# A graph layer on one core: running sums by fours, a further product per block of counts, and a subtraction on GpSimd

## The chip, the core and the metric

One core of a Trainium2 chip runs the whole layer in one launch. It has five engines that work side by side, each through its own queue in order: TensorE (PE; its weight loads are listed apart as PEld), VectorE (DVE), ScalarE (ACT), GpSimd (POOL) and SyncE (SP), which here only starts transfers. Engines wait for each other by semaphores. The metric is the device time of one execution in microseconds, lower is better; of several executions the median counts.

## What is computed

A layer of a graph network with 6250 nodes of 256 features and 106,250 directed edges `src`, `dst`, sorted by `dst`:

```
xn = layernorm(x)
x  = x + gnn(xn, edges) + mix(xn)      # mix: linear attention over all nodes
x  = x + ffn(layernorm(x))             # 8 experts, 2 per node

def graph_conv(x, edges, W0, b0, W1, b1):       # twice, relu between
    s = concatenate([edges[:, 0], edges[:, 1]])
    d = concatenate([edges[:, 1], edges[:, 0]])
    deg = maximum(segment_sum(ones_like(d), d, N), 1)
    agg = segment_sum(x[s], d, N) / deg[:, None]
    return x @ W0 + b0 + agg @ W1 + b1
```

The change lies in the part that comes first. There the edges are sorted into a table of places, from which the next stage builds the adjacency matrix block by block, and the nodes are normalised and split into a high and a low half, so that the sums over neighbours can be taken as products with the adjacency on TensorE.

## The kernel before

Nodes are cut into 49 blocks of 128 (`NB`), and twelve groups of four blocks and one of one (`NGRP`). For each block a window of 19 x 128 edges is read (`Q` = 19 columns of 128 edges). Two blocks are handled as a pair, two pairs as a batch: 13 batches, the last with one pair.

The front is one large stretch of code whose order on the engines is written out by hand: in `manual_schedule` TensorE, VectorE, ScalarE and SyncE run their instructions in the order in which Python emits them. Generators are interleaved step by step for that; a `yield` is a step. The main loop (`for b in range(NBAT)`) steps through `assign(b)` and after each of its steps takes one step of `count(b + 1)`, one of the edge preparation `edges(k)` (every other batch) and, as far as a budget goes, one of `left`, which holds the node groups `nodes(g)` and behind them the attention `mixing()`. What stands in a queue therefore depends on how many steps each generator has.

`count(b)` makes the counts of a batch. It compares the edges' keys with the numbers of the blocks (L414): `hot` is a one-hot of 100 numbers for each edge column, 19 columns per pair. It adds neighbouring columns to nine pair sums `sofar` (L423) and then runs a sum over these, eight additions of 2 x 100 elements on VectorE (L426), each reading the one before. Afterwards it issues the first three `rank_of`.

`rank_of(b, m)` puts the ranks of four (or at the end three) columns into one of three buffers `rk` in the TensorE's result memory: a product with `mark` (order within a column, and a large number at the edge's own place, L398), one or two with a matrix of ones over `sofar` (all columns before, L402), and one over the even columns of `hot` for the odd ones (L407). There are ten such counts for each full batch.

`assign(b)` takes the maximum of each count on VectorE (L438), which frees its buffer, and issues `rank_of` three further on. Then follow some small operations, and for each pair five routes (L467, comparisons into 128 x 1024 elements), four carries (L476) and their products on TensorE (L490), whose results ScalarE copies to `place`. Before the routes of each pair `own_term` is called twice (L243, products of the node group with a weight; ScalarE adds a bias, L246).

`nodes(g)` normalises a group: statistics on VectorE (L257, L260), square root on ScalarE (L265), reciprocal and offset on VectorE (L268, L269), the normalised nodes and their rounded high halves on ScalarE (L273, L276). Then come transposes on TensorE (L285), the low halves, a subtraction on VectorE (L289, normalised minus high), and the Gram products for the attention (L294). At its end the load of the group two further on is issued on SyncE's queue (L74).

GpSimd has only index patterns and the first edge loads to do in the front; the weight loads of the next stage (L642) stand in its queue behind.

Of the kernel before, what the change touches and what calls it, by code (L numbers as in the profile page):

```python
# [8 lines left out]
F32 = mybir.dt.float32  # L9
# [6 lines left out]
ENG = mybir.EngineType  # L16
PSUM = bass.MemoryType.PSUM
DRAM = bass.MemoryType.DRAM
P = 128
# [3 lines left out]
Q = 19  # L23
# [16 lines left out]
def tile_gps_layer(ctx: ExitStack, tc: tile.TileContext, a, out):  # L40
    nc = tc.nc
    x, src, dst = a["x"], a["src"], a["dst"]
    N, D = x.shape
    E = src.shape[0]
    F = a["W0_0"].shape[1]
    NE, _, FE = a["W1e"].shape
# [7 lines left out]
    J = NB + 1  # L54
# [12 lines left out]
    def blocks(g):  # L67
        return range(g * T, min(NB, g * T + T))
# [33 lines left out]
    onesb = const.tile([P, P], BF16, name="onesb")  # L102
# [32 lines left out]
    with ExitStack() as p1:  # L135
# [87 lines left out]
        if NB % 2:  # L223
            nc.vector.memset(eds[:, NP - 1, :, 1], 0)

        p1.enter_context(tc.manual_schedule(engines={ENG.PE, ENG.DVE, ENG.Activation, ENG.SP}))

        def load_nodes(g):
            load_rows(xns[g % XB][:, :, :D], blocks(g), nc.sync)
# [4 lines left out]
        def own_term():  # L234

            if not owed:
                return
            g, f, xnT = owed.pop(0)
            bs = blocks(g)
            n = len(bs)  # L240
            tp = pt1.tile([P, T * P], F32, name="tp")
            for c in range(DC):
                nc.tensor.matmul(tp[:, :n * P], w00[:, c, f * P:(f + 1) * P],  # L243
                                 xnT[:, c, :n * P], start=(c == 0), stop=(c == DC - 1))
            own = (wq, wfc)[f % 2].rearrange("p c d -> p (c d)")
            nc.scalar.activation(own[:, :n * P], tp[:, :n * P], AF.Identity, bias=bh[:, f:f + 1])  # L246
            nc.scalar.dma_start(self_d[f, :, bs[0] * P:(bs[-1] + 1) * P], own[:, :n * P])

        def nodes(g):

            bs = blocks(g)
            n = len(bs)
            xn = xns[g % XB]
            st = wk.tile([P, T, nc.vector.BN_STATS_DIM], F32, name="st")
            mv = wk.tile([P, T, nc.vector.BN_AGGR_DIM], F32, name="mv")
            for i in range(n):
                nc.vector.bn_stats(st[:, i, :], xn[:, i, :D])  # L257
                yield
            for i in range(n):
                nc.vector.bn_aggr(mv[:, i, :], st[:, i, :])  # L260
                yield
            sd = wk.tile([P, T], F32, name="sd")
            rs = wk.tile([P, T], F32, name="rs")
            off = wk.tile([P, T], F32, name="off")
            nc.scalar.activation(sd[:, :n], mv[:, :n, 1], AF.Sqrt, bias=eps)  # L265
            for _ in range(3):
                yield
            nc.vector.reciprocal(rs[:, :n], sd[:, :n])  # L268
            nc.vector.scalar_tensor_tensor(off[:, :n], mv[:, :n, 0], -1.0, rs[:, :n], op0=OP.mult,  # L269
                                           op1=OP.mult)  # L270
            yield
            for i in range(n):
                nc.scalar.activation(xn[:, i, :D], xn[:, i, :D], AF.Identity, bias=off[:, i:i + 1],  # L273
                                     scale=rs[:, i:i + 1])
            part = sent[:, bs[0]:bs[-1] + 1]
            nc.scalar.copy(part[:, :, 0], xn[:, :n, :D])  # L276
            for _ in range(5):
                yield
            while owed:
                own_term()  # L280
            xnT = wk.tile([P, DC, T * P], F32, name="xnT", bufs=1)
            for c in range(DC):
                tp = pt1.tile([P, T * P], F32, name="tp")
                for i in range(n):
                    nc.tensor.transpose(tp[:, i * P:(i + 1) * P], xn[:, i, c * P:(c + 1) * P], ident)  # L285
                nc.scalar.copy(xnT[:, c, :n * P], tp[:, :n * P])
                yield
            nc.scalar.dma_start(xnT_d[:, :, bs[0] * P:(bs[-1] + 1) * P], xnT[:, :, :n * P])
            nc.vector.tensor_sub(part[:, :, 1], xn[:, :n, :D], part[:, :, 0].bitcast(F32))  # L289
            yield  # L290

            for i, b in enumerate(bs):
                for c in range(DC):
                    nc.tensor.matmul(gram[:, GW[c]:GW[c] + W - c * P], xn[:, i, c * P:(c + 1) * P],  # L294
                                     xn[:, i, c * P:], start=False,
                                     stop=(b == NB - 1 and c == DC - 1))
                yield
            if g + XB < NGRP:
                load_nodes(g + XB)
            owed.extend((g, f, xnT) for f in range(FC))  # L300
            if g < EARLY:
                while owed:
                    own_term()
                    yield
# [77 lines left out]
        def of_batch(b):  # L382

            k, i = divmod(b, PK // PB)
            n = min(PB, NP - b * PB)
            key, pay, *rest = facts[k]
            s = slice(i * PB, i * PB + n)
            return n, key[:, s], pay[:, s], *(t[:, s] for t in rest)
# [3 lines left out]
        def rank_of(b, m):  # L392

            hot, sofar = hots[b]
            i, (q0, q1) = m // len(QS), QS[m % len(QS)]
            pp = pr.tile([P, 4, J * 2], F32, name="rk")
            h = hot[:, i].rearrange("p q j r -> p q (j r)")
            nc.tensor.matmul(pp[:, :q1 - q0], mark, h[:, q0:q1], start=True, stop=False)  # L398

            for q, d in ((2, 2),) if q0 == 0 else ((q0, 4),) if q1 - q0 == 4 else ((q0, 2), (q0 + 2, 1)):  # L400
                s, e = q // 2 - 1, max(1, d // 2)
                nc.tensor.matmul(  # L402
                    pp[:, q - q0:q - q0 + d].rearrange("p (s e) j -> p s e j", s=e), onesb,
                    sofar[:, i, s:s + e, None, :].to_broadcast([P, e, d // e, J * 2]),
                    start=False, stop=False)
            n = (q1 - q0) // 2
            nc.tensor.matmul(pp[:, 1:2 * n:2], onesb, h[:, q0:q0 + 2 * n:2], start=False, stop=True)  # L407
            ranks[b, m] = pp[:, :q1 - q0].rearrange("p q (j r) -> p q r j", r=2)

        def count(b):  # L410

            n, key, *_ = of_batch(b)
            hot = wk.tile([P, PB, Q, J, 2], BF16, name="hot")
            nc.vector.tensor_tensor(  # L414
                hot[:, :n].rearrange("p a q j r -> p (a q) j r"),
                jdx[:, None].to_broadcast([P, n * Q, J, 2]),
                key.rearrange("p a q r -> p (a q) r")[:, :, None, :].to_broadcast([P, n * Q, J, 2]),
                op=OP.is_equal)
            yield
            sofar = wk.tile([P, PB, Q // 2, J * 2], BF16, name="sofar")  # L420
            hots[b] = hot, sofar
            h = hot.rearrange("p a q j r -> p a q (j r)")
            nc.vector.tensor_add(sofar[:, :n], h[:, :n, 0:Q - 1:2], h[:, :n, 1:Q:2])  # L423
            yield
            for q in range(1, Q // 2):
                nc.vector.tensor_add(sofar[:, :n, q], sofar[:, :n, q - 1], sofar[:, :n, q])  # L426
                yield
            for m in range(min(3, n * len(QS))):
                rank_of(b, m)

        def assign(b):
# [4 lines left out]
            for m in range(n * len(QS)):  # L436
                i, (q0, q1) = m // len(QS), QS[m % len(QS)]
                nc.vector.tensor_reduce(rank[:, i, q0:q1], ranks.pop((b, m)), AX.X, OP.max)  # L438
                if m + 3 < n * len(QS):
                    rank_of(b, m + 3)  # L440
                yield
# [154 lines left out]
        for _ in nodes(0):  # L596
            pass
        first_edges = edges(0)
        for _ in nodes(1):
            next(first_edges, None)  # L600
        for _ in first_edges:
            pass
        for _ in count(0):
            pass
        left = chained(*(nodes(g) for g in range(EARLY, NGRP)), mixing())
        per_round = -(-(NGRP - EARLY) * 26 // max(1, NBAT - 2))
        for b in range(NBAT):
# [291 lines left out]
    with ExitStack() as p2:  # L899
# [36 lines left out]
        for g in range(NGRP):  # L936
            bs = blocks(g)
            n = len(bs)
# [18 lines left out]
            for i, b in enumerate(bs):  # L957
                ts = slice(i * P, (i + 1) * P)
                pb = py.tile([P, 512], F32, name="pb")
                for c in range(DC):  # L960
                    nc.tensor.matmul(pb[:, :D], xnT[:, c, ts], wmix[:, c, :],
                                     start=(c == 0), stop=False)
                for f in range(FC):
                    nc.tensor.matmul(pb[:, :D], hT[f][:, ts], w["W0_1"][:, f, :], start=False,
                                     stop=(f == FC - 1))
                nc.vector.tensor_add(bt[:, i], bt[:, i], pb[:, :D])
                pz = py.tile([P, 512], F32, name="pz")
                for f in range(FC):
                    nc.tensor.matmul(pz[:, :D], hT[f][:, ts], w["W1_1"][:, f, :], start=(f == 0),
                                     stop=(f == FC - 1))  # L970
# [67 lines left out]
    with ExitStack() as p3:  # L1038
# [200 lines left out]
        for t in range(len(steps) + AH):  # L1239
# [5 lines left out]
            if t >= AH:  # L1245
                g, j = steps[t - AH]
# [6 lines left out]
        for _ in running:  # L1253
# [37 lines left out]
                         stop=True)  # L1291
# [174 lines left out]
```

## Time and profile before

| | us |
|---|---|
| median of 3 executions (2476.81 to 2477.54) | 2476.87 |
| profiled execution | 2479.15 |
| its span, first to last instruction | 2477.5 |
| PE busy in the span | 2312.7 |
| DVE busy | 1535.1 |
| ACT busy | 991.2 |
| POOL busy | 346.9 |
| running sums L426: 96 of 2 x 100 elements, mean 0.254 | 24.4 |
| reductions L438: 100 of 4 columns, mean 0.564 | 56.2 |
| subtractions L289: 12 of 1024 elements, mean 1.219 | 14.6 |
| products L402: 75 of 400, 50 of 200, 25 of 100 columns | 48.4 |

The first rows are of the whole kernel, the last four of the front. Busy times add up the lengths of instructions; the next one of an engine can start before the end of the one before, so a mean is somewhat longer than the distance of starts. The front ends when the first comparison of the next stage (L693) starts on VectorE at 370.8 us.

### The profile page before, as it was taken

Reading aid. Unit: us, or ns where it says so; the run is one execution under the profiler, and the core shown is the slowest. Engines: PE = TensorE matmul, PEld = TensorE weight load, DVE = VectorE, ACT = ScalarE, POOL = GpSimd, SP = SyncE. Lnnn points to the kernel's source line nnn. Section 1 sums busy time; section 2 is a strip of 40 time slices with the busy share of each in tenths; the row PEclk is TensorE's granted clock in tenths of the full one; section 3 lists DMA queues with packets and bytes.
Section 4 is the critical chain, followed back from the end, with each engine's and each line's share of the span. In section 5 each row is a group of like instructions: output and inputs, shape, how many; then the busy total and the mean of one; then the engine's idle time right before and its main releaser. Section 6 shows DMA issues by size and latency. Waiting matters only on the chain. (4 is left out here: it accounts for less than half of the span.)

```text
span 2477.5 us, 44108 instructions
## 1 busy us (share of the span) xinstructions
PE 2312.7 (93%) x13401; PEld 1817.9 (73%) x13401; DVE 1535.1 (62%) x4304; ACT 991.2 (40%) x2805; POOL 346.9 (14%) x372
## 2 busy tenths in 40 slices
PE   5788869999999999989999899999999987999996
PEld 3455547777777777767777778877878766999985
DVE  5999988888888888863333334444444443655554
ACT  2344425555555555541111133333433433544443
POOL 1000000000000000000000101211121122555554
PEclk9899989999999999999999999999999987999998
DMA  3232273333333333334333264544454435778885
GB/s 107 67 102 88 83 243 131 110 107 107 110 109 112 110 110 110 111 97 172 111 124 124 88 222 160 169 153 168 160 177 148 166 111 183 230 217 244 247 250 161
DMA packets 258653, 359.24 MB, mean 145 GB/s; under 512 B 46840, under 2 KB 192895, under 8 KB 258278
## 3 DMA queue, kind: packets, MB, share of 16 engines
q1 hardware_dynamic: 229890, 302.64, 37.9%
q0 software_dynamic: 16384, 32.82, 4.0%
q10 hardware_dynamic: 12132, 20.86, 2.3%
q8 instruction: 111, 1.82, 0.3%
q14 instruction: 136, 1.11, 0.1%
HBM read 209.88 MB, written 160.00 MB: 149 GB/s over the span
## 5 line engine op out<-in xcount | busy, mean ns | idle before, releaser
L663 PE MATMUL sum<-adj,sent 128*128 128x512 f32 x2352 | 623.6, 407 | 0.0
L1077 PE MATMUL sum<-sent,adj 128*128 128x512 f32 x2401 | 580.5, 401 | 15.4 <-DVE adj L1055 14.4
L1077 PEld LDWEIGHTS sum<-sent,adj 128*128 128x128 f32 x2401 | 451.1, 190 | 125.7 <-DVE adj L1055 11.2
L714 ACT ACTIVATE adj<-pt 128x512 fp32r<-128x512 f32 (+1 forms) x637 | 359.2, 571 | 337.3 <-PE pt L711 332.2
L663 PEld LDWEIGHTS sum<-adj,sent 128*128 128x128 f32 x2352 | 420.6, 189 | 79.6
L693 DVE TENSOR_TENSOR oh<-iota,place 128x1024 bf16<-128x1024 bf16 (+1 forms) x686 | 402.1, 630 | 88.4 <-PE pt L711 86.5
L1053 ACT CAST adj<-many 128x512 fp32r<-128x512 bf16 (+1 forms) x318 | 185.5, 595 | 329.4 <-PE sum L1077 242.2
L1055 DVE CAST adj<-many 128x512 fp32r<-128x512 bf16 (+1 forms) x319 | 130.0, 414 | 247.9 <-PE sum L1077 192.7
L721 DVE CAST kept<-adj 128x512 bf16<-128x512 f32 (+1 forms) x637 | 231.7, 406 | 6.3 <-ACT adj L714 5.1
L1347 PE MATMUL pm<-yT,w 128*128 128x128 f32 x1616 | 201.9, 279 | 8.0 <-ACT yT L1331 7.3
L711 PEld LDWEIGHTS <-oh 128*128 128x128 bf16 x2548 | 148.0, 98 | 82.5 <-DVE kept L721 61.2
L711 PE MATMUL pt<-oh 128*128 128x128 bf16 x2548 | 200.1, 221 | 0.6 <-DVE misfit L633 0.6
L1347 PEld LDWEIGHTS pm<-yT,w 128*128 128x128 f32 x1616 | 191.4, 194 | 11.7 <-ACT yT L1331 10.5
L1359 PE MATMUL po<-w2e,hT 128*128 x808 | 193.9, 383 | 4.6 <-ACT hT L1351 4.6
L1359 PEld LDWEIGHTS po<-w2e,hT 128*128 128x128 f32 x808 | 147.7, 193 | 21.3 <-ACT hT L1351 5.0
L1006 POOL IOTA home_i<- 128x8 int32 x1 | 0.1, 130 | 1042.5 <-SPq L785 1042.5
L1351 ACT ACTIVATE hT<-pm,b 128x128 f32<-128x128 f32 x404 | 115.7, 372 | 50.2 <-PE pm L1347 23.1
L1210 POOL DMA_INDIRECT lists<-rows,place_i x98 | 97.1, 991 | 269.1 <-DVE rows L1202 223.0
L714 ACT ACTIVATION_READ_ACCUMULATOR adj<-pt 128x1 f32 x637 | 127.0, 199 | 0.0
L1380 POOL DMA_INDIRECT got<-ybuf,at x101 | 106.3, 1053 | 119.7 <-DMA ybuf<-res 61.7
L1363 ACT ACTIVATE res<-res,row 128x256 f32<-128x256 f32 x101 | 51.3, 508 | 163.1 <-DVE res L1362 104.9
L1395 POOL DMA_INDIRECT out_dram<-both,at x101 | 102.3, 1013 | 88.9 <-DVE both L1393 68.2
(264 smaller groups left out, 2508.9 us busy)
## 6 DMA issues: line engine op xcount, KB each, us to landing
adjd<-kept SPq DMA_DIRECT2D x588, 128.0 KB
many<-adjd SPq DMA_DIRECT2D x84, 896.0 KB
w<-in_W1e_dram SPq DMA_DIRECT2D x99, 512.0 KB
ybuf<-xn SPq DMA_DIRECT2D x1, 13440.0 KB
row<-lists SPq DMA_DIRECT2D x101, 130.5 KB
ybuf<-res SPq DMA_DIRECT2D x101, 128.0 KB
hT<-self_d SPq DMA_DIRECT2D x48, 256.0 KB
xn<-in_x_dram SPq DMA_DIRECT2D x12, 512.0 KB
```

The costliest lines, as they stand in the source:

```text
L663: nc.tensor.matmul(sums[g][c][:, :n * P], sent[:, j, k, c * P:(c + 1) * P], adj[:, :n * P], start=(first and k == 0), stop=(last and k == 1))
L693: nc.vector.tensor_tensor(oh, iota2[:, None].to_broadcast([P, m, P, 2]), place[:, j, v0:v0 + m, None, :].to_broadcast([P, m, P, 2]), op=OP ...
L711: nc.tensor.matmul(cols, o[:, :, r], o[:, :, 1 - r], start=(m == 0), stop=(m + 1 == len(todo)))
L714: nc.scalar.activation(adj[:, :n * P], pt[:, :n * P], AF.Copy, accum_out=degp[:, j, g:g + 1])
L721: nc.vector.tensor_copy(kept[:, :n * P], adjs[g, j][:, :n * P].bitcast(F32))
L1053: nc.scalar.copy(adj[:, :n * P], from_)
L1055: nc.vector.tensor_copy(adj[:, :n * P], from_)
L1077: nc.tensor.matmul(sums[g][i], adjs[s][:, i * P:(i + 1) * P], sent[:, js].rearrange("p k d -> p (k d)"), start=(js == 0), stop=(js == NB - 1))
L1347: nc.tensor.matmul(pm[:, f], w1[:, c, f * P:(f + 1) * P], yT[:, c], start=(c == 0), stop=(c == DC - 1))
L1351: nc.scalar.activation(hT[:, f], pm[:, f], AF.Relu, bias=b1[:, f:f + 1])
L1359: nc.tensor.matmul(po, hT[:, f], w2e[:, bass.ds(e, 1), f, :].rearrange("p o d -> p (o d)"), start=(f == 0), stop=(f == EC - 1))
L1380: ga = nc.gpsimd.indirect_dma_start(out=gots[t % 4], out_offset=None, in_=ybuf, in_offset=bass.IndirectOffsetOnAxis(ap=outs[t][1][:, 0:1], ...
```

## The change

Three edits, all in the front.

1. GpSimd joins the engines whose order is written out by hand, and the subtraction of the low halves is issued on GpSimd instead of VectorE.
2. `sofar` no longer holds a running sum at every place. One addition over four places at once adds each even pair sum to the odd one behind it, so that odd places hold sums of four columns; three more additions run over the odd places. Even places keep their plain pair sum. `rank_of` adds the sum up to the block (odd place before it) to all its columns, and in a further product the pair sum of its first two columns to the rest.
3. `count` gets eight empty steps before its first three `rank_of`. With four additions fewer it has 14 steps in place of 10.

```diff
-        p1.enter_context(tc.manual_schedule(engines={ENG.PE, ENG.DVE, ENG.Activation, ENG.SP}))
+        p1.enter_context(tc.manual_schedule(
+            engines={ENG.PE, ENG.DVE, ENG.Activation, ENG.SP, ENG.Pool}))
...
-            nc.vector.tensor_sub(part[:, :, 1], xn[:, :n, :D], part[:, :, 0].bitcast(F32))
+            nc.gpsimd.tensor_sub(part[:, :, 1], xn[:, :n, :D], part[:, :, 0].bitcast(F32))
...
-            for q, d in ((2, 2),) if q0 == 0 else ((q0, 4),) if q1 - q0 == 4 else ((q0, 2), (q0 + 2, 1)):
-                s, e = q // 2 - 1, max(1, d // 2)
-                nc.tensor.matmul(
-                    pp[:, q - q0:q - q0 + d].rearrange("p (s e) j -> p s e j", s=e), onesb,
-                    sofar[:, i, s:s + e, None, :].to_broadcast([P, e, d // e, J * 2]),
-                    start=False, stop=False)
+            if q0:
+                nc.tensor.matmul(pp[:, :q1 - q0], onesb,
+                                 sofar[:, i, q0 // 2 - 1, None, :].to_broadcast([P, q1 - q0, J * 2]),
+                                 start=False, stop=False)
+            nc.tensor.matmul(pp[:, 2:q1 - q0], onesb,
+                             sofar[:, i, q0 // 2, None, :].to_broadcast([P, q1 - q0 - 2, J * 2]),
+                             start=False, stop=False)
...
-            for q in range(1, Q // 2):
-                nc.vector.tensor_add(sofar[:, :n, q], sofar[:, :n, q - 1], sofar[:, :n, q])
+
+            fours = sofar[:, :n, 1:Q // 2:2]
+            nc.vector.tensor_add(fours, sofar[:, :n, 0:Q // 4 * 2:2], fours)
+            yield
+            for q in range(3, Q // 2, 2):
+                nc.vector.tensor_add(sofar[:, :n, q], sofar[:, :n, q - 2], sofar[:, :n, q])
+                yield
+
+            for _ in range(8):
                 yield
```

## The prediction

> **What bounds the kernel now.** I began with the busy time of each engine in stretches cut by hand, because the change touches only the front, the first 371 us; the 726 us behind it are shown for contrast. Columns: stretch and length, then busy time and instructions of TensorE (PE), its weight loads, VectorE (DVE), ScalarE, GpSimd (POOL), the granted TensorE clock, DMA share and GB/s.
>
> ```profile
> 0.00:51.00 51.00, 26.87 (x85) 15.72 (x86) 24.51 (x73) 14.88 (x24) 8.78 (x19) 0.97 0.43 120
> 51.00:86.00 35.00, 23.56 (x173) 15.46 (x172) 34.50 (x96) 7.94 (x29) 0.00 (x0) 0.85 0.16 47
> 86.00:100.00 14.00, 13.52 (x83) 8.29 (x82) 10.58 (x22) 7.04 (x12) 0.00 (x0) 1.00 0.34 126
> 100.00:116.00 16.00, 10.44 (x72) 6.32 (x72) 15.93 (x50) 4.79 (x25) 0.00 (x0) 0.68 0.12 28
> 116.00:128.00 12.00, 11.66 (x63) 7.14 (x62) 9.77 (x21) 4.98 (x8) 0.00 (x0) 1.00 0.35 131
> 128.00:187.00 59.00, 49.40 (x377) 31.09 (x375) 58.62 (x142) 24.96 (x89) 0.00 (x0) 0.96 0.30 94
> 187.00:206.00 19.00, 17.15 (x105) 10.71 (x103) 15.14 (x41) 7.58 (x21) 0.00 (x0) 0.94 0.31 103
> 206.00:298.00 92.00, 76.54 (x550) 50.54 (x550) 89.13 (x220) 36.80 (x116) 0.00 (x0) 0.93 0.23 80
> 298.00:311.00 13.00, 12.19 (x71) 7.25 (x69) 8.51 (x21) 5.66 (x12) 0.00 (x0) 1.00 0.29 102
> 371.00:1097.00 726.00, 724.51 (x4913) 561.47 (x4913) 610.11 (x1332) 389.72 (x1283) 2.24 (x3) 1.00 0.34 111
> ```
>
> The front has two kinds of stretch. In 51-86, 100-116, 128-187 and 206-298 (202 us) VectorE works 198 us: it sets the time. In 86-100, 116-128, 187-206 and 298-311 (58 us) TensorE works 54.5 and VectorE 44: VectorE runs into a wait there, 3.3, 2.2, 3.7 and 4.4 us long in its timeline. GpSimd is empty. Behind 371 us TensorE works 724.5 of 726, and nothing of that stage is edited: what the front wins or loses should arrive at the end whole.
>
> Next the groups of the front (line, engine, operation, tiles, shapes, count; busy us, mean ns; idle before) and the waits of TensorE:
>
> ```profile
> L426 DVE TENSOR_TENSOR sofar<-sofar 128x200 bf16<-128x200 bf16 x96 | 24.4, 254 | 0.3
> L289 DVE TENSOR_TENSOR sent<-xn,sent 128x1024 fp32r<-128x1024 f32 x12 | 14.6, 1219 | 6.1 <-ACT sent L276 6.1
> PE rk L398 <- DVE rank L438: 30.3, 45, 1.7
> ```
>
> These two groups are what leaves VectorE. Their means overlap with the next operation, so I use distances of starts, from the timeline of VectorE (start, length):
>
> ```profile
> 189.09 0.57 DVE L438 TENSOR_REDUCE rank<-rk 128x8 f32<-128x400 f32 x1
> 189.57 0.25 DVE L426 TENSOR_TENSOR sofar<-sofar 128x200 bf16<-128x200 bf16 x1
> 189.74 0.57 DVE L438 TENSOR_REDUCE rank<-rk 128x8 f32<-128x400 f32 x1
> ```
>
> A reduction occupies 0.48 us (189.09 to 189.57), a running sum 0.17. The subtraction (L289) started at 190.77 and its follower at 191.91: 1.14 us. The pair sum over 1800 elements (L423) started at 183.98, its follower at 184.98: 1.00 us.
>
> **Running sums.** A batch of two blocks' pairs has eight additions of 200 elements, 8 x 0.17 = 1.36 us. They become one addition of 800 elements and three of 200. The new one lies between the rows of 200 (0.17) and 1800 (1.00): 0.17 + 600/1600 x 0.83 = 0.48. After: 0.48 + 3 x 0.17 = 0.99, a gain of 0.37 per batch. Batch 0 falls in the start, where TensorE's first counts come at 50.82 us behind its own products whatever VectorE does; 11 full batches and a half one remain: 11 x 0.37 + 0.33 = **4.4 us off**. If the new addition should cost as much as four small ones (0.68), the gain is 0.17 a batch, 2 us; if as little as one (0.17), 8 us.
>
> **Added product.** Three of the five counts of a block get a further product of 200 columns, the fifth 100 more columns: 75 products and 25 wider ones. TensorE's timeline gives 0.09 us between starts for 200 columns and 0.17 for 400; in stretches of lower clock twice that (187.99 to 188.33 for 400). So a full count costs 0.17 + 0.17 + 0.09 + 0.09 = 0.52 us, or 1.0 at the low clock, and all additions come to 6.7 + 1.0 = 8 us, 15 at worst. Cover: the 30.3 us in which the first product of a count waits for a reduction (row above). Without it they would be on the path: reductions that stand alone follow each other at 0.48 us, less than 0.52, so in that part TensorE and VectorE are about equal at full clock, and TensorE leads by 0.5 us a count at the low one. I put 0 for it, bounds 0 and +5 (some five counts a batch by 0.5 in about two of twelve batches of low clock).
>
> **Eight more steps before the next batch's first counts.** The three counts of the next batch are put on TensorE four steps later, in the built order behind the first own-term products in most batches, and in some behind the transposes. They used to stand in front of them, held up by the last reductions: 0.15 to 0.19 us of idle time before 84.70 and 85.35, while own terms started only at 86.33. The own terms, which the four TensorE stretches hang on, start about 0.5 us earlier, less the 0.25 us of added products among the counts that still lie in that stretch: 4 x 0.25 = **1.0 us off**, bounds 0 and 4 (the whole 1 us of the three counts). What is late instead, the counts, is needed only a whole batch of routes (18 us) later.
>
> **Subtraction on GpSimd.** 13 go. The two at the start gain nothing (50.82 again: VectorE then waits 7 instead of 2 us for the first count). Those at 89.89, 118.30, 190.77 and 302.80 lie in TensorE's stretches: there a VectorE that is 1.14 us faster waits 1.14 us longer. Seven remain (67.48, 142.90, 168.09, 219.04, 243.75, 266.88, 290.72): 7 x 1.14 = 8.0 us off. Its result is read only behind 371 us; the load of nodes two groups ahead (SP) waits for GpSimd now instead of VectorE, but also for the Gram products, which end some 8 us after the old subtraction (190.77 against 198.6). The edge loads queued behind it are as early as before. GpSimd's own queue has nothing behind the subtractions but the weight loads of the next stage, after 347 us of idle time.
>
> No row of before has a GpSimd subtraction. Nearest is its copy of the same 1024 elements (L1108), one operand, seen beside VectorE's casts:
>
> ```profile
> 1480.80 1.61 DVE L1055 CAST adj<-many 128x512 fp32r<-128x512 bf16 x2
> 1480.95 1.18 POOL L1108 COPY rows<-rows 128x1024 f32<-128x1024 f32 x1 [1.77 <-DVE rows L1105]
> 1579.46 0.76 DVE L1055 CAST adj<-many 128x512 fp32r<-128x512 bf16 x2
> 1579.62 1.51 POOL L1108 COPY rows<-rows 128x1024 f32<-128x1024 f32 x1 [2.04 <-DVE rows L1105]
> 1530.04 1.04 POOL L1108 COPY rows<-rows 128x1024 f32<-128x1024 f32 x1 [2.37 <-DVE rows L1105]
> ```
>
> Alone the copy takes 1.04 us. Against two casts back to back it takes 1.51 and the casts keep their 0.76; once the copy got in between, and the casts took 1.61, 0.85 more. One of the two always stands still. With two operands I take twice the copy, 2.1 us. What that costs VectorE is bounded by 0 (it never stops for it) and 2.1 a piece; I take 1.5 where it begins among routes and carries (2.1 less the 0.4 of the operation then under way and the 0.15 by which VectorE resumed before the copy's end), and 1.0 where it begins among the reductions, which stand between the additions and may run meanwhile. Going by ScalarE's copies (L276, ended at 66.6, 142.1 and 283.3 among routes, 165.5, 214.6, 241.0 and 263.7 among reductions) that is 3 x 1.5 + 4 x 1.0 = 8.5 against 8.0: **0.5 us on**, bounds -8.0 and 7 x 2.1 - 8.0 = +6.7.
>
> The Trainium skill speaks against this edit. "SBUF — State Buffer", section "Who interferes with whom", says that a VectorE instruction with two SBUF inputs and a GpSimd instruction that reads SBUF exclude each other, and that the second to issue blocks until the first is done. No row of before shows this for a VectorE operation of two inputs, only for the cast. "GPSIMD Engine Reference", section 3.1, gives 4497 ns for an addition of 2048 elements; half of it, an estimate, is 2.25 us instead of 2.1, and the part would cost 1 us more. Were the exclusion only for casts, the part would be worth the full 8.0.
>
> **Sum.** -4.4 (sums) + 0 (products) - 1.0 (order) + 0.5 (GpSimd) = -4.9 us. The profiled execution took 2479.15 us (span 2477.5 and 1.65 around it), so 2474.25; it lies 2.28 above the median of 2476.87, so the median becomes **2472.0 us**.
>
> **The rivals.** A measurement of this kernel tells 0.2%, 5 us, from no change; the limits are 2471.9 and 2481.8.
> B, *GpSimd works beside VectorE for nothing*. For it: nine of twelve copies left the casts untouched. Against it: each copy then waited itself, and in the front VectorE has hardly a gap. -4.4 - 1.0 - 8.0 = -13.4: 2463.5.
> C, *the subtraction stops VectorE each time* (the slower side). Place: routes, carries, one-hots and running sums, all operations of two tensors. From 8.0 + 5.4 = 13.4 us in seven stops, 1.9 each, it eats all gains. It decides if in addition those in TensorE's stretches count, because VectorE delivers the carries late there: 10 x 2.1 = 21 against 13.4: +7.6, or 2484.5. For it: the 1.61 above. Against it: VectorE's 2 to 4 us of waiting in just those stretches.
> D, *TensorE becomes the bound of the counts*. The reductions wait for 0.52 us (low clock: 1.0) counts; the sums gain nothing, and 5 us come on: 0 + 5 - 1.0 + 0.5 = +4.5 at worst; with half of the 5 it is +2.0: 2478.9. For it: a granted clock of 0.68 in 100-116. Against it: three of ten counts leave that part.
>
> **How the numbers follow.** Forecast 0.42 (own range 2468 to 2477), B 0.25, C 0.18, D 0.15. The range goes from B's 2463 to 2483, leaving out C's upper half and what is better than B. Faster by over 0.2%: all of B, nearly half of the forecast, 0.44; slower: C, two thirds of it, the end of D and of the forecast, 0.20; within: 0.36.
>
> **What would show it.** Right: VectorE's last work of the front (now 370.8 us) ends some 5 us earlier; the sums' group has four members a batch and 0.99 us; GpSimd's subtractions show 2 us or more, and a route, carry or sum beside them shows 1 to 2 us in place of 0.69, 0.56 or 0.25. Wrong: those stay at their lengths (B); reductions show idle time before them put down to the counts (D); the stage behind 371 us changes its 726 us; or the subtraction takes far over 2.1 us.

## The result and the profile after

The changed kernel is slower: a median of 2482.18 us over 15 executions, against 2476.34 us for the kernel before, timed beside it 15 times. The ratio is 1.003, with a 95% interval of 1.0022 to 1.0039, so 5.4 to 9.7 us more. The forecast was 2472.0. 2482.18 lies inside the range that was given (2463 to 2483), but the sign is wrong.

The profiled execution took 2483.37 us (span 2481.7). First the busy times by stretch, cut at the same work as before (columns as in the prediction: length, TensorE, its weight loads, VectorE, ScalarE, GpSimd, granted clock, DMA share, GB/s).

```profile
51.40:86.70 35.30, 23.97 (x176) 16.87 (x175) 34.31 (x85) 7.59 (x29) 5.97 (x1) 0.82 0.16 43
86.70:101.70 15.00, 14.63 (x91) 9.15 (x90) 11.73 (x24) 7.12 (x13) 2.61 (x1) 0.97 0.32 121
131.00:190.00 59.00, 48.96 (x374) 31.39 (x373) 58.62 (x130) 24.79 (x84) 4.45 (x2) 0.97 0.27 85
212.00:310.00 98.00, 83.21 (x542) 53.19 (x540) 87.98 (x202) 38.05 (x119) 12.60 (x5) 0.87 0.21 73
381.30:1107.40 726.10, 724.57 (x4913) 561.44 (x4914) 609.80 (x1331) 389.40 (x1284) 2.24 (x3) 1.00 0.34 111
```

VectorE has fewer instructions in its stretches (85 for 96 in the first, 202 for 220 in the last but one) and is busy for as long. GpSimd, empty there before, now has one subtraction or more in each of the front's four. The front ends at 381.3 us, where it ended at 370.8: 10.5 us later. The stage behind it still takes 726 us, and 10.8 us are still there at 2049 us. Of these the last stage gave back some 6.6 us in this pair of executions: the execution of before had a wait of 4.62 us of TensorE for ScalarE at 2459 us, that of after has none there above 0.93. That stage is not edited, and why its waits differ was not settled; the ratio comes from all executions.

The groups of the front (line, engine, operation, tiles, shapes, count; busy us, mean ns; idle before), the routes of before first, then four groups of after:

```profile
L467 DVE TENSOR_TENSOR route<-iota,slot 128x1024 bf16<-128x1024 bf16 x100 | 64.1, 679 | 10.2 <-PE rt L490 9.9
L476 DVE TENSOR_TENSOR route<-iota,slot 128x1024 bf16<-128x1024 bf16 x100 | 70.1, 741 | 8.9 <-PE rt L499 8.6
L290 POOL TENSOR_TENSOR sent<-xn,sent 128x1024 fp32r<-128x1024 f32 x12 | 34.4, 2867 | 237.8 <-ACT sent L277 237.8
L432 DVE TENSOR_TENSOR sofar<-sofar 128x200 bf16<-128x200 bf16 x36 | 12.2, 339 | 0.1
L429 DVE TENSOR_TENSOR sofar<-sofar 128x800 bf16<-128x800 bf16 x12 | 10.2, 846 | 0.0
```

The 48 additions of the sums take 22.4 us, hardly less than the 96 of before (24.4). An addition of 200 elements has a mean of 0.339 us for 0.254, a route 0.741 for 0.679. Nothing about these operations was changed: some of them have become much longer. Which ones is seen in the timeline (start, length) of GpSimd, then of VectorE, in the first full batch:

```profile
66.36 5.97 POOL L290 TENSOR_TENSOR sent<-xn,sent 128x1024 fp32r<-128x1024 f32 x1 [24.64 <-ACT sent L277]
...
68.41 1.89 DVE L476 TENSOR_TENSOR route<-iota,slot 128x1024 bf16<-128x1024 bf16 x3
70.22 0.42 DVE L258 BATCH_NORM_STATS2 st<-xn 128x6 f32<-128x256 f32 x1
70.55 2.33 DVE L476 TENSOR_TENSOR route<-iota,slot 128x1024 bf16<-128x1024 bf16 x1
```

The subtraction starts at 66.36 among routes and carries that follow each other without a gap, and gets nowhere. At 70.22 VectorE has a statistics operation, with one operand; there the subtraction gets in. The next route, at 70.55, takes 2.33 us instead of some 0.7: the subtraction ends at 66.36 + 5.97 = 72.33, and the route 0.55 us later, at 72.88. That is the stop, 1.6 us here.

### The profile page after: what moved, and what is told of

Its sections match the earlier page's. It is cut to its first block, busy times and chain, and to the rows that moved or that the text cites. A ratio compares the mean times of both kernels' runs of the same rounds, so it can differ in the third digit from the quotient of the medians.

```text
span 2481.7 us, 44216 instructions
## 1 busy us (share of the span) xinstructions
PE 2322.7 (94%) x13476; PEld 1826.2 (74%) x13476; DVE 1536.5 (62%) x4239; ACT 989.4 (40%) x2805; POOL 382.9 (15%) x385
```

## The experiments

The front is compared batch by batch, as the difference of starts of the one-hot (`hot`, the comparison at L414 in before) on VectorE, one per batch. It is counted from the first count on TensorE (48 to 52 us), which varies with the loads at the start. The last interval ends with the first comparison of the next stage. The table is worked out from the timelines; "ten" is the change against before of the sum of the first ten intervals. The eleventh is left out of it, since TensorE waits in it for a load of weights for the mixing, up to 3.4 us, differently in each execution.

Where VectorE sets the time, an interval repeats to a few hundredths (24.97 or 24.98 us in the first interval of the five kernels in which VectorE has the same work there: before, e3, e6, e8 and e11). Where it waits for TensorE it does not: in e8, in which no operation of VectorE is more than 0.04 us longer than in before, interval 7 is 1.47 us shorter, 8 and 10 are 0.71 and 1.67 longer, the last two at a granted clock of 0.93 and 0.94 for 1.00. Each trace is one execution. So a difference under about 1.5 us in one of these three intervals, or about 1 us in the sum of ten, says something only where several kernels share it.

Where GpSimd works in the front (e2, e4, e8, e9), it also stands in the list of the first edit, and in e1 and e5 it is taken out of it; the diffs below do not show that line.

```
intervals (us)                                                             sum   ten
before 24.98 27.45 28.49 23.64 26.06 27.48 28.12 23.27 26.22 27.83 26.72 29.74 320.0    0
after  25.12 28.89 27.78 24.11 26.41 27.37 30.48 25.29 27.86 30.18 27.21 29.78 330.5  +9.9
e1     24.60 28.51 27.60 23.26 25.68 28.34 28.44 22.75 25.84 28.68 28.74 29.78 322.2  +0.2
e2     25.83 27.46 28.49 24.45 27.50 28.18 28.29 25.60 28.31 29.19 26.64 29.23 329.2  +9.8
e3     24.98 27.56 28.57 23.64 26.06 28.04 28.40 23.44 26.21 28.26 29.91 29.85 324.9  +1.6
e4     25.44 27.36 28.34 24.10 27.91 28.86 28.60 26.10 28.38 30.94 31.58 29.78 337.4 +12.5
e5     24.59 28.46 28.19 23.25 25.68 28.05 28.39 23.62 25.90 28.61 31.29 29.77 325.8  +1.2
e6     24.97 27.45 27.34 23.63 26.05 27.45 27.60 23.13 26.21 27.89 25.74 29.28 316.7  -1.8
e8     24.97 27.45 28.48 23.64 26.05 27.67 26.65 23.98 26.27 29.50 28.31 29.12 322.1  +1.1
e9     26.95 27.44 28.49 25.58 28.03 30.71 29.89 25.58 28.52 28.24 28.28 29.34 337.1 +15.9
e10    24.48 27.45 28.48 22.58 24.91 26.96 26.77 24.03 25.25 26.93 26.57 29.81 314.2  -5.7
e11    24.97 28.66 28.57 23.63 26.05 27.46 28.01 23.14 26.20 27.89 25.96 28.45 319.0  +1.0
```

**e1, e2 and e3: each part by itself.** e1 is the changed kernel with the subtraction back on VectorE:

```diff
-            nc.gpsimd.tensor_sub(part[:, :, 1], xn[:, :n, :D], part[:, :, 0].bitcast(F32))
+            nc.vector.tensor_sub(part[:, :, 1], xn[:, :n, :D], part[:, :, 0].bitcast(F32))
```

> The changed kernel with the subtraction back on VectorE; sums by fours, added product and eight steps stay. The front ended at 370.8 us before and at 381.3 after. Port theory (each GpSimd subtraction stops VectorE 1.6 to 1.9 us in place of 1.14 us of work, and that is all of the loss): the front ends at 366 to 369, ratio to before 0.997 to 0.999. TensorE theory (the added product makes the counts late, 19.0 us of waiting of the reductions in place of 6.2): the front still ends at 376 to 380, ratio 1.001 to 1.003, and the reductions still wait some 17 us. Both halves: in between, 370 to 374.

Measured: 2469.51 us beside 2473.02, ratio 0.9988 (0.9979 to 0.9997); ten intervals +0.2.

e2 is the opposite, the kernel before with only the subtraction moved to GpSimd:

```diff
-            nc.vector.tensor_sub(part[:, :, 1], xn[:, :n, :D], part[:, :, 0].bitcast(F32))
+            nc.gpsimd.tensor_sub(part[:, :, 1], xn[:, :n, :D], part[:, :, 0].bitcast(F32))
```

> The kernel before with nothing but the subtraction on GpSimd. Port theory: VectorE operations of two tensors beside the subtractions are stretched by 1.6 to 1.9 us, eleven times; the front ends 4 to 6 us later, 375 to 377, ratio 1.0015 to 1.0035. TensorE theory: 8 to 12 us of VectorE work are gone and nothing comes instead, front at 360 to 366, ratio 0.996 to 0.998.

Measured: ratio 1.0031 (1.0019 to 1.0043), ten intervals +9.8. This one edit carries the whole loss of after (1.003, +9.9). How it does so has two forms. In intervals 1 and 4 the subtraction falls among routes and carries, and they grow by 0.85 and 0.81 us. In 8 and 9 it falls among the sums and reductions, and they grow by 2.33 and 2.09. The timeline of e2 there, GpSimd and VectorE, then TensorE (in brackets idle time before, and what ended it):

```profile
245.22 2.31 POOL L290 TENSOR_TENSOR sent<-xn,sent 128x1024 fp32r<-128x1024 f32 x1 [23.44 <-ACT sent L277]
...
245.90 1.75 DVE L427 TENSOR_TENSOR sofar<-sofar 128x200 bf16<-128x200 bf16 x1
...
250.74 0.57 DVE L439 TENSOR_REDUCE rank<-rk 128x8 f32<-128x400 f32 x1 [0.57 <-PE rk L408]
```

```profile
248.19 0.33 PE L399 MATMUL rk<-hot,mark 128*128 128x400 bf16 x1 [1.63 <-DVE rank L439]
248.36 0.49 PE L403 MATMUL rk<-sofar,onesb 128*128 128x400 bf16 x1
...
249.66 0.54 PE L399 MATMUL rk<-hot,mark 128*128 128x400 bf16 x1
```

A sum of 0.25 us takes 1.75. The reduction behind it is late, TensorE idles 1.63 us for the buffer, and its products of 400 columns then grow from 0.33 to 0.54 us apiece, as in stretches of a lower clock (over interval 8 the granted clock is 0.93, in before 1.00); a reduction at 250.74 waits 0.57 us for them. So a stop at this place costs more than the stop itself; how much of it is the clock is not known, since e8 has the same 0.93 there without stops and is 0.71 longer.

e3 is the kernel before with a further product of 200 columns of zeros (`nil`) in three of five counts, as many columns as the change adds there:

```diff
+            if 0 < q0 < 16:
+                nc.tensor.matmul(pp[:, 2:4].rearrange("p q (k j) -> p (q k) j", k=5), onesb,
+                                 nil[:, None, :].to_broadcast([P, 10, J * 2 // 5]),
+                                 start=False, stop=False)
```

> The kernel before with one more product of 200 columns (of zeros) in three of five counts, which is the added TensorE work alone. Port theory: hidden in the 30 us in which the counts wait for reductions, front at 370 to 372, ratio 0.9995 to 1.0005. TensorE theory: the reductions wait longer by 5 to 9 us, front at 375 to 380, ratio 1.002 to 1.004.

Measured: ratio 1.0005 (0.9994 to 1.0016), ten intervals +1.6 (its 29.91 is the late load). Five of the ten stay within 0.1 us, among them 1, 4, 5 and 9; intervals 6, 7 and 10 grow by 0.56, 0.28 and 0.43. So the product is covered in about half of the batches and not in all.

**e4, e5, e6 and e11: the order.** The number of empty steps is varied: e4 is the changed kernel with four for eight, e5 is e1 with four for eight, e6 is the kernel before with four steps added and nothing else, e11 the same with eight. Since the changed sums have four steps fewer, `count` has 10 steps in before, e4 and e5, 14 in after, e1 and e6, and 18 in e11. The diff is that of e6:

```diff
             for q in range(1, Q // 2):
                 nc.vector.tensor_add(sofar[:, :n, q], sofar[:, :n, q - 1], sofar[:, :n, q])
                 yield
+            for _ in range(4):
+                yield
```

> The changed kernel with four empty steps in place of eight, so that the next batch's counts stand where they stood before the change. Port theory and TensorE theory: steps are worth at most 1 us in either direction, front at 380 to 384, ratio 1.002 to 1.004. Order theory (the counts moved behind the own terms keep TensorE busy when the reductions need it): front at 372 to 377, ratio 1.000 to 1.002.

> Subtraction on VectorE, sums by fours and added product, but four empty steps, so that the next counts stand where they stood before. With eight steps the ratio was 0.9988, and batches took 0.4 us less where VectorE sets the time but 0.3 to 1.1 us more in three of four batches with a TensorE stretch. If the moved counts cause that surplus: batches as before less 0.4, front 2 to 4 us earlier than with eight steps, ratio 0.997 to 0.999. If the steps are what pays for the added product: slower than with eight, ratio 1.000 to 1.002.

> The kernel before with four more empty steps, so that the next counts stand where the change puts them, and nothing else. Mine (order worth 1 us): ratio 0.999 to 1.000. If the moved counts harm the TensorE stretches: 1.0005 to 1.0015, with the surplus in the batches that hold a wait of VectorE for L490 or L265.

> The kernel before with eight more empty steps, the next counts four steps later still than with four (ratio 0.998). If what helps is that TensorE starts the own terms without waiting for the last reductions, four steps already give all of it: ratio 0.9975 to 0.9985, batches within 0.3 us of those with four steps. If later is better by itself: 0.996 to 0.997. If the counts now collide with the products of the routes: 0.9985 to 1.000.

Measured: e4 1.0058 (1.0044 to 1.0071); e5 0.9994 (0.9984 to 1.0003); e6 0.998 (0.9969 to 0.9991), 2469.14 us beside 2474.97; e11 0.9993 (0.9984 to 1.0002). Four steps alone, which take nothing away from any engine, are the best version that was run of those that compute the layer, about 5 us under the kernel before. e4 is slower than any of its expectations. Eight steps alone can't be told from none.

TensorE's timeline tells why. In before the next batch's counts stand in front of the own terms, which start at 115.74 in the third batch; the chain that VectorE's routes wait for hangs on them. In e6 the order there is:

```profile
113.45 3.66 PE L243 MATMUL tp<-xnT,late 128*128 128x512 f32 x8
116.95 0.33 PE L398 MATMUL rk<-hot,mark 128*128 128x400 bf16 x1
...
118.90 3.70 PE L243 MATMUL tp<-xnT,late 128*128 128x512 f32 x8 [0.60 <-ACT wq L246]
```

The first half of the own terms no longer waits for reductions, the counts lie between the halves, where TensorE would wait for ScalarE in any case (0.60 us of it are left), and VectorE's wait for the route products falls from 2.2 to 1.1 us: the 1.15 us of interval 3. In after, which also has 14 steps, the counts stand at the same place, here in the second batch:

```profile
86.09 4.48 PE L244 MATMUL tp<-xnT,late 128*128 128x512 f32 x8
90.41 0.33 PE L399 MATMUL rk<-hot,mark 128*128 128x400 bf16 x1
...
91.77 3.62 PE L244 MATMUL tp<-xnT,late 128*128 128x512 f32 x8
```

So e6 against before is the change's own order, taken by itself: -1.8 in ten intervals. The same four steps give -1.0 between e5 and e1 and -2.5 between e4 and after. In e11 the counts come later than in the change, here again in the second batch:

```profile
85.18 3.66 PE L243 MATMUL tp<-xnT,late 128*128 128x512 f32 x8
90.52 3.70 PE L243 MATMUL tp<-xnT,late 128*128 128x512 f32 x8 [1.68 <-ACT wq L246]
...
95.49 0.33 PE L398 MATMUL rk<-hot,mark 128*128 128x400 bf16 x1
```

The hole between the halves stands empty for 1.68 us, and the counts lie behind the transposes, ahead of the Gram and route products: VectorE waits 4.5 us for these, 3.3 before, and interval 2 grows by 1.21.

**e9 and e10: the two sides of the move, one at a time.** e9 keeps VectorE's subtraction and adds one on GpSimd for each group but the last, started by the same copy of ScalarE. It has the size of the next group, so eleven are of the same size and the twelfth has a quarter of it (its result, put into the next group's places, is overwritten there):

```diff
             nc.vector.tensor_sub(part[:, :, 1], xn[:, :n, :D], part[:, :, 0].bitcast(F32))
+            if g + 1 < NGRP:
+                nb = blocks(g + 1)
+                nc.gpsimd.tensor_sub(sent[:, nb[0]:nb[-1] + 1, 1], xn[:, :len(nb), :D],
+                                     part[:, :len(nb), 0].bitcast(F32))
```

> The kernel before, VectorE's subtraction kept, with a subtraction of the same size added on GpSimd (reading the same nodes, writing the low halves of the next group, which VectorE overwrites later): the price of the stops alone, with nothing taken off VectorE. Port theory: eleven to twelve stops of 1.6 to 1.9 us and the TensorE stretches as cover, front 12 to 19 us later than 370.8, ratio 1.005 to 1.008. If the loss with the subtraction on GpSimd had come from a late load of nodes behind it and not from stops: ratio 0.999 to 1.001.

Measured: ratio 1.0068 (1.0046 to 1.0089); the whole front +17.1, ten intervals +15.9. Its timeline, GpSimd and VectorE:

```profile
66.51 2.40 POOL L293 TENSOR_TENSOR sent<-xn,sent 128x1024 fp32r<-128x1024 f32 x1 [25.10 <-ACT sent L277]
...
66.31 3.03 DVE L481 TENSOR_TENSOR carry<-hot,pay 128x800 bf16<-128x800 bf16 x2
...
194.94 2.17 POOL L293 TENSOR_TENSOR sent<-xn,sent 128x1024 fp32r<-128x1024 f32 x1 [23.33 <-ACT sent L277]
...
195.25 1.98 DVE L431 TENSOR_TENSOR sofar<-sofar 128x200 bf16<-128x200 bf16 x1
```

Two carries take 3.03 us, with nothing beside them 1.05 (e8 below): 1.98 more, and interval 1 is 1.97 longer than in before; 4 and 5 by 1.94 and 1.97. Intervals 2 and 3, where VectorE waits for TensorE, stay as they are to 0.01 us. Interval 6, which has such a wait too, grows by 3.23: its stop falls on a sum, ahead of the counts and everything behind them.

e10 takes the subtraction off VectorE and puts it nowhere; ScalarE, which has time, makes a copy instead. It leaves out the low halves, which then hold the rounded nodes once more, so its result is not that of the layer:

```diff
-            nc.vector.tensor_sub(part[:, :, 1], xn[:, :n, :D], part[:, :, 0].bitcast(F32))
+            nc.scalar.copy(part[:, :, 1], xn[:, :n, :D])
```

> The kernel before without the subtraction: the low halves are filled with a copy by ScalarE instead (so the messages are the rounded halves twice, not high and low), which takes the 1.14 us per group off VectorE and puts nothing on GpSimd. The prediction counted seven groups at 1.14 us, 8.0 us: batches without a TensorE stretch 1.14 us shorter, ratio 0.9965 to 0.9975. If a subtraction among the reductions only filled a wait for the next count (as the batches with GpSimd's work there, 2.1 to 2.3 us longer instead of 0.84, suggest), only the batches where it stands among the routes gain: 3 to 5 us, ratio 0.998 to 0.999.

Measured: 2463.74 us beside 2470.3, ratio 0.9965 (0.9951 to 0.9979), which is 8.6 us (5.2 to 12.1); ten intervals -5.7. Intervals 4 and 5 give 1.06 and 1.15, 2 and 3 nothing, and 8 is 0.76 longer, at a granted clock of 0.93 for 1.00. The two sides add up: -5.7 and +15.9 make +10.2, and e2, which has both, shows +9.8.

**e8: what of GpSimd's work stops VectorE.** For each group ten index patterns of 128 numbers on GpSimd, which are only written, nothing being read for them, started by a copy of one element:

```diff
+            nc.gpsimd.tensor_copy(jmp[:, :1].bitcast(F32), part[:, 0, 0, :1].bitcast(F32))
+            for _ in range(10):
+                nc.gpsimd.iota(jmp, pattern=[[1, P]], base=0, channel_multiplier=-1)
```

> The kernel before, VectorE's subtraction kept, with ten index patterns of 128 elements on GpSimd (each some 0.25 us, writing only) behind each ScalarE copy of the high halves, started by a copy of one element. If a GpSimd instruction stops VectorE because both read SBUF: no stop, VectorE's routes, carries and sums keep 0.69, 0.72 and 0.26 us at most, ratio 0.999 to 1.001. If any GpSimd work of 2 us does it: stops of up to 2 us, ratio 1.004 to 1.008.

Measured: ratio 1.0 (0.9989 to 1.0011). The same place of the first batch in its timeline:

```profile
66.40 2.97 POOL L293 IOTA jmp<- 128x128 int32 x10
...
65.72 1.05 DVE L480 TENSOR_TENSOR carry<-hot,pay 128x800 bf16<-128x800 bf16 x2
```

GpSimd works for 2.97 us among routes and carries, longer than a subtraction that gets through, and no route of the front takes more than 0.707 us, no sum more than 0.265. Writing alone, in instructions of 0.236 us, stops nothing, and neither does GpSimd's place in the list of the first edit. A GpSimd instruction of this length that reads one operand was not tried in the front.

## Why the prediction was wrong, term by term

**The subtraction (predicted +0.5, measured +9.8 in ten intervals): the step that failed is the price of a stop.** The gain of the move was put at 8.0: e10 shows 5.7 in ten intervals and 8.6 (5.2 to 12.1) by its ratio, so it was not much too high. The length of GpSimd's instruction was put at 2.1 and is 2.17 us where it runs unhindered. The stops were put at 1.5 us among routes and 1.0 among reductions, 8.5 in seven places. Measured in e9, intervals 1, 4 and 5 cost 1.94 to 1.97 each, 7, 8 and 9 cost 1.77 to 2.31, 10 costs 0.41 (its subtraction is the one of a quarter's size): 12.7 in the seven. Two steps of that working fail. The 0.4 and 0.15 us taken off for the operation under way and for an early resumption were read from a copy beside casts and do not hold here. And "may run meanwhile" is true of the reductions, but useless: behind a few of them stands a sum or another operation of two tensors, which waits for the rest of the subtraction, and the counts behind it wait too. The third step that fails is smaller: of the places in TensorE's stretches, taken as covered, two are (0.00 and -0.01 us), but that of interval 6 is not (+3.23); in the fourth e9 has no GpSimd subtraction. 12.7 + 3.2 = 15.9 in place of 8.5.

The rival C had the mechanism, 1.9 us a stop, and the side; its total of +7.6 was reached by ten stops of 2.1, where the runs show eight, most of them near 2 and one above 3. What was said against it, VectorE's own waits in TensorE's stretches, was true of two stretches. B is excluded by the first stretched route.

The Trainium skill had spoken against the edit: "SBUF — State Buffer", "Who interferes with whom", says that a VectorE instruction with two SBUF inputs and a GpSimd instruction that reads SBUF exclude each other, and that one which only writes does not. e9 (carries 1.98 us longer) and e8 (no route above 0.707) show just this. The estimate of 2.25 us from "GPSIMD Engine Reference", section 3.1, was close to the 2.17 measured as well; only the stop, not the length, was under-priced.

**The sums (predicted -4.4) and the added product (predicted 0, bounds 0 and +5).** The sums did what was worked out. After's timeline of VectorE shows the new addition and its follower:

```profile
80.32 0.57 DVE L429 TENSOR_TENSOR sofar<-sofar 128x800 bf16<-128x800 bf16 x1
80.80 0.42 DVE L258 BATCH_NORM_STATS2 st<-xn 128x6 f32<-128x256 f32 x1
```

0.48 us between starts, as predicted. e1 and e6 have the same 14 steps and differ in sums and product alone: intervals 1, 4, 5, 8 and 9 are 0.37 or 0.38 shorter in e1, for a predicted 0.37. But 2, 3, 6, 7 and 10 are longer, by 1.06, 0.26, 0.89, 0.84 and 0.79, and over ten intervals the sums and the product together cost 2.0 us, where 4.4 were to be won. e5, which has them with before's 10 steps, shows +1.2, and intervals 2, 6, 7 and 10 longer by 1.01, 0.57, 0.27 and 0.78 as well; by the ratios e5 can't be told from before. Against a saving of 3.7 in ten batches the product so took, by estimate, 4.9 to 5.7 us, at the upper bound of what was given and not the 0 that was put in the sum: this is the second step that failed. About 1 us of it, that of interval 2, goes with a granted clock of 0.87 there in e1 and e5 for 0.94 in before; e3 and e4, which have the product too, have 0.94 and are 0.11 longer and 0.09 shorter. Whether the product brings the lower clock is not known. The product was mis-sized: it takes cover that was counted on. After's timeline of TensorE shows it, at a low clock (0.68 granted from 78 to 86 us):

```profile
83.42 0.54 PE L399 MATMUL rk<-hot,mark 128*128 128x400 bf16 x1
83.75 0.54 PE L402 MATMUL rk<-sofar,onesb 128*128 128x400 bf16 x1
84.09 0.37 PE L405 MATMUL rk<-sofar,onesb 128*128 128x200 bf16 x1
84.25 0.37 PE L409 MATMUL rk<-hot,onesb 128*128 128x200 bf16 x1
84.42 0.54 PE L399 MATMUL rk<-hot,mark 128*128 128x400 bf16 x1
```

A count takes 1.00 us (83.42 to 84.42), while a reduction alone takes 0.48: here TensorE sets the pace. The waits of VectorE say the same, before and after (us in all, times, longest):

```profile
DVE rank L438 <- PE rk L407: 6.2, 6, 2.1
```

```profile
DVE rank L447 <- PE rk L409: 19.0, 14, 6.1
```

Of the 19.0, 6.1 is the first count at the start; e1, without the stops, has 9.2. So rival D is right in part: it decides in some batches and by the traces eats more than the sums save, but the kernel is not measurably slower by it (e5 0.9994, 0.9984 to 1.0003; with the steps, e1, 0.9988).

**The order (predicted -1.0, bounds 0 and -4): right in sign and near in size, but not as it was worked out.** The four steps of the change give -1.8 in e6, with a ratio of 0.998. The own terms do start earlier, by more than the 0.5 us that were assumed: in e6's second batch 9.01 us behind the one-hot, in before 10.53, and in the third 9.24 behind 12.49. But the gain was to come from four TensorE stretches at 0.25 us each, and it comes from one of them, interval 3 with 1.15 (the granted clock of 0.94 there, 0.82 in before, is not the reason: e3 and e8 have 0.94 too and gain nothing). In 2, 6 and 10 the difference is 0.06 at most; in interval 2 the Gram products start 19.26 us behind the one-hot in both kernels, since the counts, now between the halves, take the time that was won. That the sum came out near is partly luck. "Needed only a whole batch of routes later" holds for 14 steps and not for 18: in e11 the counts stand ahead of the Gram and route products and leave a hole of 1.68 us, and it shows +1.0 and a ratio of 0.9993 that is open to both signs.

The terms of the trace add up: e6 (-1.8), e1 less e6 (+2.0) and e2 (+9.8) make +10.0; after shows +9.9 in ten intervals, 10.5 over the front. That they agree to 0.1 us is chance, as the 1.1 of e8 says. Of the 15 us between the forecast's -4.9 and this, the subtraction has 9.3 and the product with the sums 6.4; the order was 0.8 better. By the ratio after loses 7.4 us, e2 alone 7.7. That the ratios give some 2 us less than the traces in these two, and more gain than the traces in e6 and e10, was not settled; the intervals of the ratios are about that wide, and each trace is one execution.

Of the signs of an error that had been named, two came: reductions show idle time put down to the counts, and the subtraction takes more than 2.1 us, 2.867 in the mean, because it waits itself. The 726 us of the next stage did not move, and the routes and sums did not keep their lengths. Of the signs that were to speak for the forecast, these stretched operations and the sums of four members a batch came; the earlier end of the front did not.

## What to carry to other kernels

Work moved from a bound engine to an idle one is free only if the idle engine does not take something from the bound one: on this chip a GpSimd subtraction with two operands cost VectorE 1.98 us to save it 1.14, so price the stop at the whole length of the GpSimd instruction, and look at what is queued behind the place where it falls. Where an engine follows another closely, weigh a saving on one against the added work on the other at the clock that the profile grants there, not at full speed. The order in a queue is worth trying by itself: work that is not needed soon belongs into a hole that another wait leaves, neither ahead of the critical product nor far behind the hole; four empty steps gave 0.2%, with eight no gain could be told.

## What the runs showed of the hardware that was not expected

GpSimd can be the one that waits, for long: in after the subtraction took 5.97 us at 66.36 and 5.19 at 290.98, instead of 2.17. The first got in beside an operation of VectorE with one operand, the second in a gap of 0.04 us behind the last carry; then VectorE's next operation with two operands stood still (the one-hot at 294.16 took 4.00 us for 2.14). It is not always so: in e9 the subtraction at 66.51 got in between two carries without a gap and took 2.40. What decides that is open. It is not only additions and comparisons of two tensors that stand: operations with a scalar and two tensors do too, in after at 167.43 (2.17 us, 0.31 with GpSimd idle) and here, with the reductions in front of it running free:

```profile
189.81 2.39 DVE L447 TENSOR_REDUCE rank<-rk 128x8 f32<-128x400 f32 x5
192.23 1.33 DVE L459 SCALAR_TENSOR_TENSOR room<-own,rank 128x76 f32<-128x76 bf16 x1
...
191.30 2.17 POOL L290 TENSOR_TENSOR sent<-xn,sent 128x1024 fp32r<-128x1024 f32 x1 [21.87 <-ACT sent L277]
```

Five reductions, which read TensorE's result memory, take 2.39 us, 0.48 each as always, though the subtraction starts during them; the operation after them, 0.24 us with GpSimd idle, takes 1.33 and ends as the subtraction does.
